# Another written order for the steps of the fused attention and feed-forward stage

## The chip, the cores and the metric

The kernel runs on one core of one Trainium2 chip. The metric is the device time of one execution in microseconds (us), as the median over several executions. A core has five engines that matter here: TensorE (PE in the profile; its weight loads stand apart as PEld), VectorE (DVE), ScalarE (ACT), GpSimd (POOL) and SyncE (SP, which issues DMAs). Each engine takes its instructions in the order in which they are written, and waits on semaphores for what the others produce.

## The reference

The input is one sequence of 2048 tokens with 128 channels. Four layers follow each other, each on the normalized sum so far: an oscillatory state space layer, a mixture of eight experts, a causal attention with 16 heads of 8 channels, and a block of six sub-layers of windowed attention and feed-forward. The last block takes two thirds of the time, and the change lies in it. Cut to what matters:

```python
def attn_layer(x, Wqkv, qs, ksc, Wo):            # HEADS 16, DIM_HEAD 64, WINDOW 32
    q, k, v = jnp.split(x @ Wqkv, 3, -1)         # then split into heads
    q = l2norm(q) * qs
    k = l2norm(k) * ksc
    q = q * cos * scale + rotate_half(q) * sin * scale
    k = k * cos * inv + rotate_half(k) * sin * inv
    out = local_attention(q, k, v)               # softmax over own and previous window of 32
    return out @ Wo

def ffn_layer(x, g, bln, W1, b1, W2, b2):
    xn = layernorm(x) * g + bln
    a, gate = jnp.split(xn @ W1 + b1, 2, -1)     # 341 channels each
    return a * gelu(gate) @ W2 + b2

for i in range(DEPTH):                           # DEPTH 6
    x = attn_layer(shift_tokens(x), ...) + x
    x = ffn_layer(shift_tokens(x), ...) + x
```

## The kernel before

The kernel has three earlier stages, which the change leaves alone, and `stage4`, which holds the six sub-layers. Stage 4 keeps the sequence transposed on the chip (channels on partitions, tokens along the free dimension) in two buffers, `s4[0]` and `s4[1]`, and cuts it into 16 tiles of 128 tokens. With six sub-layers that makes 96 tiles, numbered through by `t`. The work on a tile is cut into named steps, and every step is a small function. Some belong to each tile, some to each pair of tiles (`px0` to `px3`, `s`), some to each group of four (the feed-forward steps), and some to each sub-layer (`mm`, `mc0`, `mc1`).

The steps of a tile, in the order in which the data flows, with the engine that does each:

- `tab` (POOL): table of rotary factors. `ps00`, `ps01` (PE): the queries into a PSUM buffer of two banks; `ps10`, `ps11`: the keys into another.
- On the queries' buffer: `ra0` and `rb0` (DVE, multiply with the tables), `sq0` (ACT, squares). On the keys' buffer: `ra1`, `rb1`, `sq1`. `ss0`, `ss1` (DVE): sums of the squares. `rs0`, `rs1` (POOL): add the two rotary halves. `rn` (POOL, 12 small instructions): inverse norms. `kn` (POOL): scale the keys.
- `pt0`, `pt1` (PE): transpose queries and keys. `qT`, `kT` (ACT): copy them out of PSUM. `ca` (ACT): hand the last window of keys to the next tile.
- `sc0` to `sc3` (PE): scores. `sm`, `mx` (DVE): add the mask, negated row maxima. `nb` (POOL): scale these. `ex0`, `ex1` (ACT, eight exponentials each). `su`, `rc` (DVE): row sums and reciprocals. `nr` (POOL): scale. `tr` (DVE): transpose in blocks.
- `z0`, `z1` (PE): weights times inputs. `zc0`, `zc1` (ACT): copy out. `px0` to `px3` (PE, per pair): times the product of the value and output matrices, which `mm` (PE) and `mc0`, `mc1` (ACT) make once a sub-layer. `s` (DVE): add to the sequence.
- Per group of four tiles: `xk`, `xkc` transposed inputs for `z`; `xt`, `xs`, `fr`, `xn`, `xu`, `xb` the normalization; `ph00` to `ph21` (PE), `ge0` to `ge2` (ACT), `act0` to `act2` (DVE), `py0` to `py2` (PE) the feed-forward; `s2` (DVE) adds to the sequence; `st` stores, in the last sub-layer.

What sets the order is the list `steps`. It gives each step a lateness in units of one tile. Step `name` of tile `t` becomes a job at `t + lateness`; all jobs are sorted by that number and called one after the other:

```python
                    jobs.append((t + late, job))
            for _, job in sorted(jobs, key=lambda j: j[0]):
                job()
```

The engines' objects are wrapped (`InOrder`, line 67), so that no scheduler moves an instruction afterwards. For that reason nearly every instruction of stage 4 stands under line 67 in the profile, and is told apart by the tiles that it writes and reads. Steps by their tiles in the profile: `ra`: rot_a<-big,tab; `rb`: rot_b<-big,tab; `sq`: sq<-big; `ss`: ss<-sq; `ex`: sm<-sm,mx,rn; `rs`: rot_a<-rot_a,rot_b; `s`: s<-s,big; `sc`: big<-kT,qT; `z`: big<-at,xw; `px`: big<-zs,vo; `ps`: big<-wqk,s.

Three things tie the engines to this order beyond the data itself.

- PSUM buffers: the function `big` hands out four buffers of two banks, in the order in which they became free in the written order. `ps00`, `ps10`, `pt0`, `pt1`, `sc0`, `z0` (two), `px0` and the feed-forward steps take one each, and wait on the chip until the former user's last reader is done. A key buffer is held until its third reader (`sq`, `ra` or `rb`) is done.
- Readers of one PSUM buffer on different engines are put in the written order by semaphores: two reads of the same buffer by DVE and ACT do not overlap. In the order before, `sq0` is written after `ra0` and `rb0`, and its instruction waits for `rb0`; `rb1` is written after `sq1`, and waits for it.
- The remainder of stage 3: four jobs `left0` to `left3` at 1.2, 2.2, 3.1 and 3.4 finish tiles 4 to 7 of the sequence. The weights of sub-layer `l` are loaded by a job at `16 l - 3.5`, and the value and output matrices of the next one by the step `mm`.

Of the kernel before, what the change touches and what calls it, by code (L numbers as in the profile page):

```python
# [94 lines left out]
class Kernel:  # L95
# [885 lines left out]
    def stage4(self, x3, out):  # L981
        nc, tc, a = self.nc, self.tc, self.a
        with ExitStack() as ctx:
# [36 lines left out]
            st = [{} for _ in range(DEPTH * NT + 1)]  # L1020
# [426 lines left out]
            def of(f, *n):  # L1447
                return lambda t: f(t, *n)

            tiles = dict(  # L1450
                tab=tab, rn=rn, kn=kn, pt0=of(pt, 0), qT=qT, pt1=of(pt, 1), kT=kT, ca=ca, sm=sm,
                mx=mx, nb=nb, su=su, rc=rc, nr=nr, tr=tr,
# [11 lines left out]
            for n in range(3):  # L1464
# [6 lines left out]


            steps = [
                ("tab", 3.450), ("ps00", 4.422), ("ps01", 4.422), ("ra0", 4.460), ("rb0", 4.460), ("ps10", 4.543),
                ("ps11", 4.637), ("sq0", 4.715), ("sq1", 4.734), ("rb1", 4.919), ("ra1", 4.991), ("rs0", 5.208),
                ("ss1", 5.244), ("rs1", 5.279), ("ss0", 5.300), ("rn", 5.300), ("kn", 5.300), ("pt0", 5.484),
                ("qT", 5.484), ("pt1", 5.756), ("kT", 5.756), ("sc0", 6.172), ("sc1", 6.179), ("sc2", 6.179),
                ("sc3", 6.223), ("sm", 6.309), ("mx", 6.309), ("nb", 6.420), ("ca", 6.444), ("ex0", 7.153),
                ("ex1", 7.319), ("su", 7.446), ("rc", 7.719), ("xk", 7.750), ("xkc", 7.783), ("nr", 7.950),
                ("tr", 8.007), ("z0", 8.275), ("z1", 8.300), ("zc0", 8.364), ("zc1", 8.416), ("mm", 8.893),  # L1480
                ("px0", 9.005), ("px1", 9.005), ("px2", 9.005), ("px3", 9.160), ("mc1", 9.257), ("s", 9.267),
                ("mc0", 9.438), ("xt", 13.584), ("xs", 13.584), ("fr", 13.623), ("xn", 13.956), ("xu", 14.168),
                ("xb", 14.168), ("ph00", 14.404), ("ph01", 14.404), ("ge0", 14.404), ("ph10", 14.891),
                ("ph11", 14.891), ("ge1", 14.905), ("ph20", 14.917), ("ph21", 14.919), ("act0", 14.921),
                ("ge2", 14.924), ("py0", 15.002), ("act1", 15.154), ("act2", 15.165), ("py1", 15.394),
                ("py2", 15.394), ("s2", 15.415), ("st", 15.500),
            ]
            last = DEPTH * NT
            jobs = [(1.2, left0), (2.2, left1), (3.1, left2), (3.4, left3)]
# [126 lines left out]
```

## Time and profile before

| what | us |
|---|---|
| median of three executions | 2426.61 (2423.41 to 2428.54) |
| profiled execution, device time | 2425.9 |
| its span on the core | 2424.2 |
| first PE instruction of stage 4 | 782.1 |
| first `ps00` (tile 0) | 797.0 |
| `ra0` of tile 4, 16 and 95 | 850.8, 1043.7, 2340.5 |
| last add into the output | 2419.8 |
| one sub-layer in the steady part (16 tiles) | 262.8 |

In the second to fifth sub-layer every 16 tiles take 262.8 us, so a tile takes 16.43 us. The busy time of each engine in these 262.8 us: PE 246.9, DVE 222.0, ACT 209.3, POOL 201.1. Overlapping records are counted once, so that busy and idle time add up. The granted TensorE clock over the span is 0.95, and 0.98 in the steady part. DMA moves little there (its share is 0.04 at most).

How to read the views: the "windows" view gives the busy time of each engine in a stretch and, in brackets, the number of instructions. The groups of instructions give the busy time, the mean duration of one in nanoseconds, then the idle time of the engine just before them with who ended it. The timeline gives start, duration, engine and tiles.

### The profile page before, as it was taken

To read this page: it belongs to the slowest core of one execution; us is meant where nothing else is said; L and a number is where in the kernel's file an instruction comes from. 1 tells how busy PE (TensorE), PEld (TensorE's weight loads), DVE (VectorE), ACT (ScalarE), POOL (GpSimd) and SP (SyncE) were. 2 spreads that over 40 slices of the span, in tenths; PEclk is the share of its full clock that TensorE was granted. 3 is DMA by queue.
4 is the path that set the end of the run, shared out by engine and by line. 5 is a ranking of instruction groups with operands and counts; after the bars stand their busy time and mean duration, and the time that the engine had idled before them with its cause. 6 is when DMAs were issued, how large, how long until landed. Compare 5 with 4: busy or idle time off the path is not lost.

```text
span 2424.2 us, 61787 instructions
## 1 busy us (share of the span) xinstructions
PE 2158.5 (89%) x26188; PEld 1240.8 (51%) x26188; DVE 1880.0 (78%) x2808; ACT 1643.0 (68%) x3221; POOL 1394.1 (58%) x2122
## 2 busy tenths in 40 slices
PE   4677889999998699999998999999999999899997
PEld 3563333333333365556555655656555655555564
DVE  7666768777663688888888888888888888888873
ACT  3322445666665488788777877778878877787773
POOL 4244310011011688777777777777877777777770
PEclk8888989999998799999999999999999999999998
DMA  2000000000001000000000000000000000000000
GB/s 74 1 1 1 1 1 2 2 2 2 2 1 63 3 19 1 13 10 25 4 2 21 19 11 2 21 2 28 2 10 13 25 5 2 2 2 1 6 6 9
DMA packets 14134, 25.38 MB, mean 10 GB/s; under 512 B 1657, under 2 KB 10530, under 8 KB 13090
## 3 DMA queue, kind: packets, MB, share of 16 engines
q1 hardware_dynamic: 13276, 20.97, 2.7%
q8 instruction: 206, 3.38, 0.6%
q10 hardware_dynamic: 582, 0.46, 0.1%
q14 instruction: 70, 0.57, 0.1%
HBM read 20.37 MB, written 1.05 MB: 9 GB/s over the span
## 4 chain that ended last, share of the span: by engine, by line
PE 49%; DVE 33%; ACT 8%; issue 5%; POOL 4%; DMA 0%; POOLq 0%; DVEq 0%; ACTq 0%
PE big L67 31%; PE sc L67 9%; DVE mx L67 6%; DVE rot_a L67 5%; DVE rot_b L67 5%; PE av L67 5%; ACT sq L67 4%; DVE ss L67 3%; DVE sm L67 2%; DVE su L67 2%; DVE at L67 2%; DVE s L67 1%; ACT sm L67 1%; DVE act L67 1%; PE py L67 1%
## 5 line engine op out<-in xcount | busy, mean ns | idle before, releaser
L67 ACT ACTIVATE sm<-sm,mx,rn 128x64 f32<-128x64 f32 x1536 | 522.9, 436 | 0.3
L67 POOL TENSOR_TENSOR rot_a<-rot_a,rot_b 128x1024 f32<-128x1024 f32 x192 | 451.9, 2365 | 24.2 <-DVE rot_a L67 18.8
L67 DVE TENSOR_REDUCE mx<-sc 128x1 f32<-128x512 f32 (+3 forms) x640 | 354.9, 604 | 124.2 <-PE sc L67 117.2
L67 ACT ACTIVATE ex<-sc 128x512 f32<-128x512 f32 (+3 forms) x640 | 302.5, 536 | 204.2 <-PE sc L67 200.9
L67 PE MATMUL big<-wqk,s 128*128 128x512 f32 x768 | 374.7, 606 | 3.2 <-DVE sm L67 3.2
L67 PE MATMUL big<-zs,vo 128*128 128x256 f32 x1536 | 342.4, 381 | 16.2 <-ACT sq L67 14.8
L67 DVE TENSOR_TENSOR rot_b<-big,tab 128x1024 f32<-128x1024 f32 x192 | 234.2, 1220 | 143.8 <-ACT sq L67 142.3
L67 PEld LDWEIGHTS big<-zs,vo 128*128 128x128 f32 x1536 | 288.2, 190 | 58.7 <-ACT sq L67 19.5
L67 PE MATMUL sc<-qT,kT 32*128 32x512 bf16 (+3 forms) x1920 | 248.5, 353 | 24.6 <-DVE mx L67 16.3
L67 DVE TENSOR_TENSOR rot_a<-big,tab 128x1024 f32<-128x1024 f32 x192 | 233.7, 1217 | 44.1 <-PE big L67 43.4
L67 ACT ACTIVATE sq<-big 128x1024 f32<-128x1024 f32 x192 | 186.1, 1021 | 111.1 <-DVE rot_b L67 111.1
L67 PE MATMUL big<-at,xw 32*128 32x512 f32 x1536 | 233.7, 685 | 24.5 <-DVE at L67 24.4
L67 PEld LDWEIGHTS big<-ident,rot_a 128*128 128x128 f32 x1536 | 174.9, 141 | 139.9 <-POOL rot_a L67 63.3
L67 ACT COPY zs<-big 128x1024 f32<-128x1024 f32 x192 | 186.2, 1009 | 82.5 <-PE big L67 82.5
L67 PE MATMUL sc<-kT,qT 32*128 32x512 bf16 (+3 forms) x1920 | 232.3, 359 | 1.6 <-DVE krest L67 0.5
L67 PE MATMUL big<-ident,rot_a 128*128 128x128 f32 x1536 | 203.1, 275 | 33.8 <-POOL rot_a L67 29.1
L67 DVE TENSOR_REDUCE ss<-sq 128x16 f32<-128x1024 f32 x192 | 226.1, 1198 | 1.4
L67 POOL TENSOR_TENSOR sm<-sm,su 128x1024 f32<-128x1024 f32 x96 | 182.6, 1902 | 61.5 <-DVE su L67 61.5
L67 PEld LDWEIGHTS big<-wqk,s 128*128 128x128 f32 x768 | 135.2, 194 | 154.2 <-issue 139.5
L67 POOL TENSOR_SCALAR_AFFINE_SELECT ex<-ex 128x512 f32<-128x512 f32 x64 | 40.6, 635 | 272.3 <-ACT ex L67 272.0
L67 POOL TENSOR_TENSOR rot_a<-rot_a,rn 128x1024 f32<-128x1024 f32 x96 | 182.6, 1903 | 7.5
L67 PE MATMUL av<-ex,va 128*32 128x256 f32 (+1 forms) x2432 | 180.6, 378 | 4.9 <-POOL ex L67 3.5
(236 smaller groups left out, 3353.4 us busy)
## 6 DMA issues: line engine op xcount, KB each, us to landing
wqk<-in_L_ffn_Wqkv SPq DMA_DIRECT2D x12, 512.0 KB, 5.2
wvo<-in_wvo SPq DMA_DIRECT2D x6, 1024.0 KB, 5.5
w<-in_L_ffn_W SPq DMA_DIRECT2D x6, 341.0 KB, 7.2
x<-in_L_attn_hidden_states SPq DMA_DIRECT2D x4, 256.0 KB, 4.3
out<-act SPq DMA_DIRECT2D x4, 256.0 KB, 2.7
rot<-in_rot SPq DMA_DIRECT2D x1, 960.0 KB, 7.2
w<-in_L_ffn_W SPq DMA_DIRECT2D x12, 64.0 KB, 1.8
qks<-in_qks SPq DMA_DIRECT2D x6, 128.0 KB
```

The costliest lines, as they stand in the source:

```text
L67: return self._tc.keep_in_program_order(call(*args, **kw))
```

## The change

Only the list `steps` differs: the same 72 steps with other latenesses. No function, tile, instruction or DMA is added or removed; their order on each engine changes, and with it who waits for whom and which PSUM buffer is reused after which.

```diff
             steps = [
-                ("tab", 3.450), ("ps00", 4.422), ("ps01", 4.422), ("ra0", 4.460), ("rb0", 4.460), ("ps10", 4.543),
-                ("ps11", 4.637), ("sq0", 4.715), ("sq1", 4.734), ("rb1", 4.919), ("ra1", 4.991), ("rs0", 5.208),
-                ("ss1", 5.244), ("rs1", 5.279), ("ss0", 5.300), ("rn", 5.300), ("kn", 5.300), ("pt0", 5.484),
-                ("qT", 5.484), ("pt1", 5.756), ("kT", 5.756), ("sc0", 6.172), ("sc1", 6.179), ("sc2", 6.179),
-                ("sc3", 6.223), ("sm", 6.309), ("mx", 6.309), ("nb", 6.420), ("ca", 6.444), ("ex0", 7.153),
-                ("ex1", 7.319), ("su", 7.446), ("rc", 7.719), ("xk", 7.750), ("xkc", 7.783), ("nr", 7.950),
-                ("tr", 8.007), ("z0", 8.275), ("z1", 8.300), ("zc0", 8.364), ("zc1", 8.416), ("mm", 8.893),
-                ("px0", 9.005), ("px1", 9.005), ("px2", 9.005), ("px3", 9.160), ("mc1", 9.257), ("s", 9.267),
-                ("mc0", 9.438), ("xt", 13.584), ("xs", 13.584), ("fr", 13.623), ("xn", 13.956), ("xu", 14.168),
-                ("xb", 14.168), ("ph00", 14.404), ("ph01", 14.404), ("ge0", 14.404), ("ph10", 14.891),
-                ("ph11", 14.891), ("ge1", 14.905), ("ph20", 14.917), ("ph21", 14.919), ("act0", 14.921),
-                ("ge2", 14.924), ("py0", 15.002), ("act1", 15.154), ("act2", 15.165), ("py1", 15.394),
-                ("py2", 15.394), ("s2", 15.415), ("st", 15.500),
+                ("tab", -0.681), ("ps00", 0.000), ("ps01", 0.000), ("ra0", 0.049), ("sq0", 0.094), ("ss0", 0.186),
+                ("ps10", 0.205), ("ps11", 0.205), ("rb0", 0.219), ("sq1", 0.231), ("rb1", 0.231), ("ra1", 0.451),
+                ("rs0", 0.508), ("rs1", 0.561), ("ss1", 0.636), ("rn", 0.646), ("kn", 0.975), ("pt0", 1.054),
+                ("qT", 1.153), ("pt1", 1.490), ("kT", 1.505), ("ca", 1.688), ("sc0", 1.700), ("sc1", 1.875),
+                ("sc2", 1.907), ("sc3", 1.907), ("sm", 1.907), ("mx", 1.907), ("nb", 1.907), ("ex0", 2.171),
+                ("ex1", 2.935), ("su", 2.962), ("rc", 3.040), ("nr", 3.297), ("tr", 3.529), ("xk", 3.637),
+                ("xkc", 3.755), ("z0", 3.917), ("z1", 3.917), ("zc1", 3.988), ("zc0", 4.005), ("px0", 5.266),
+                ("px1", 5.453), ("mm", 5.620), ("mc1", 5.621), ("px2", 5.648), ("mc0", 5.681), ("px3", 6.291),
+                ("s", 6.475), ("xt", 11.567), ("xs", 11.976), ("fr", 12.088), ("xn", 12.298), ("xu", 12.664),
+                ("xb", 12.856), ("ph00", 13.295), ("ph01", 13.505), ("ge0", 13.539), ("act0", 13.542),
+                ("ph10", 13.556), ("ph11", 13.580), ("ph20", 13.620), ("ph21", 13.621), ("ge1", 13.630),
+                ("act1", 13.630), ("ge2", 13.631), ("py0", 13.643), ("py1", 13.645), ("act2", 13.813),
+                ("py2", 14.008), ("s2", 14.394), ("st", 14.494),
             ]
```

Folded into one tile's turn, and leaving out the steps that belong to groups, the orders on DVE and ACT are these; a number behind a step says how many tiles it lags behind the newest tile.

```
DVE before: su-3 ra0 rb0 rc-3 rb1 ra1 tr-3 ss1 ss0 sm-1 mx-1      (s-4 in every second turn, between ss1 and ss0)
DVE after:  rc-3 ra0 ss0 rb0 rb1 ra1 tr-3 ss1 sm-1 mx-1 su-2      (s-6 in every second turn, behind ra1)
ACT before: ca-2 qT-1 sq0 sq1 kT-1 ex0-2 ex1-2 zc0-3 zc1-3
ACT after:  zc0-4 sq0 qT-1 ex0-2 sq1 kT-1 ca-1 ex1-2 zc1-3
```

In the program as built after the change, `sq0` waits for `ra0`, `ss0` waits for `sq0`, and `rb1` waits for `sq1`. The first tiles' steps start at lateness 0 instead of 3.45, so that `left0` to `left3` stand between the steps of tiles 0 to 3, where they stood ahead of the first `tab` before.

## The prediction

> **What bounds the kernel now.** First the windows view: the stretch, its length, busy us and records of PE, PEld, DVE, ACT, POOL, the granted clock, DMA share, GB/s. The first row holds tiles 0 to 15, the second a steady sub-layer.
>
> ```profile
> 797.00:1041.00 244.00, 213.95 (x2805) 134.31 (x2803) 195.94 (x215) 179.67 (x344) 189.25 (x277) 0.92 0.03 11
> 1304.00:1567.00 263.00, 247.08 (x3117) 155.93 (x3114) 222.14 (x268) 209.26 (x398) 201.31 (x294) 0.98 0.04 12
> ```
>
> No engine is full: of 262.8 us PE is idle for 16 and DVE for 41. What bounds a tile's turn is therefore a ring of waits, and I count it on DVE, where each idle stretch has a named cause. The groups of DVE in that sub-layer show them (busy, mean ns, idle before, by whom):
>
> ```profile
> L67 DVE TENSOR_TENSOR rot_b<-big,tab 128x1024 f32<-128x1024 f32 x32 | 39.0, 1219 | 23.4 <-ACT sq L67 23.1
> L67 DVE TENSOR_TENSOR rot_a<-big,tab 128x1024 f32<-128x1024 f32 x32 | 38.9, 1217 | 7.1 <-PE big L67 7.0
> L67 DVE TENSOR_REDUCE ss<-sq 128x16 f32<-128x1024 f32 x32 | 37.7, 1198 | 0.2
> L67 DVE TENSOR_TENSOR s<-s,big 64x256 f32<-64x256 f32 x16 | 6.7, 420 | 8.4 <-PE big L67 8.3
> ```
>
> Per tile (divide by 16): `rb1` waits 1.46 for `sq1`, `ra0` 0.44 and `s` 0.52 for PE, `ss` next to nothing. DVE works 222.14/16 = 13.88 and stands 2.54: 16.43 a tile. Then the timeline, to see why `rb1` waits:
>
> ```profile
> 1386.16 1.02 ACT L67 COPY qT<-big 128x1024 f32<-128x1024 f32 x1
> 1390.42 2.77 ACT L67 ACTIVATE sm<-sm,mx,rn 128x64 f32<-128x64 f32 x8
> ...
> 1421.77 1.22 DVE L67 TENSOR_TENSOR rot_b<-big,tab 128x1024 f32<-128x1024 f32 x1
> 1423.02 1.94 ACT L67 ACTIVATE sq<-big 128x1024 f32<-128x1024 f32 x2 [1.79 <-DVE rot_b L67]
> 1425.06 1.23 DVE L67 TENSOR_TENSOR rot_b<-big,tab 128x1024 f32<-128x1024 f32 x1 [1.92 <-ACT sq L67]
> ```
>
> `rb0` ends at 1422.99 and ACT, idle for 1.79 although PE is long done with that buffer, starts `sq0` 0.03 later; both squares end at 1424.96 and `rb1` starts 0.10 later. So DVE and ACT take turns on the queries' and keys' buffers, in the written order, and every hand-over is paid in full. Before, ACT does both squares in one go between them.
>
> **The ring after the change.** It takes this apart. DVE runs `ra0 ss0 rb0 rb1`, and `ss0` needs `sq0`, which now waits for `ra0`. ACT runs `sq0 qT ex0 sq1`: eight exponentials and a copy now stand between the two squares, and `rb1` waits for the second. From the end of `ra0`, with back-to-back costs (two squares take 1.94, so the first costs 0.92; by the same overlap `qT` costs 0.92 and `ex0` 2.67):
> - `sq0` starts at 0.03 and ends at 1.05, `ss0` starts at 1.15: DVE stands 1.15.
> - `rb1` starts at 0.03 + 0.92 + 0.92 + 2.67 + 1.02 + 0.10 = 5.66. DVE has only `ss0` and `rb0` for that time, 1.13 + 1.22 from 1.15 on, so it is done at 3.50 and stands 2.16.
>
> That is 3.31 standing in place of `rb1`'s 1.46. The 0.96 for PE at `ra0` and `s` I cost at nothing, because DVE is now the later one: counted from `ra0`, a plain turn is 1.22 + 5.66 to `rb1`, then seven DVE steps at 1.16 and `rc`, 15.2 in all; `z` can end at about 14 (`tr` ends at 10.3, `sc` and `z` take 1.4 and 1.9 by their starts in the timeline), and `px3`, which `s` needs, is issued a turn's fraction ahead. If that cover went, 0.96 a tile would return. With 0.07 for record overlap that a wait undoes: 13.88 + 3.31 + 0.07 = 17.26.
>
> **The turn with the feed-forward** (one in four). `ph10` takes the PSUM buffer that `ra1` reads last, free at 9.2 in that turn. Behind it on PE stand `ph11`, `ph20`, `ph21`, `py0`, `py1` and then `sc`: six steps at 0.85 (four `ps` records cover 1.71 to the next start) and 1.4, so `sc` ends at 15.7. DVE reaches `sm` after `rb1 ra1 s tr act0 act1 ss1 act2`, at 14.4. It waits 1.3, or 0.33 per tile. Queued behind it are `mx`, `su`, `rc` and the next `ra0`. Once a sub-layer `mm` (2.06 on PE) and `mc1` now fall into such a turn; between 0 (hidden) and 2.8/16 = 0.18 I take 0.15, as everything behind `ph11` stands on the path there. Sum 17.74.
>
> **The clock.** The rows show 0.98 while PE's longest idle stretches are 1.7 us, and 0.92 in the filling stretch where they are longer. After, PE stands about 3 us ahead of `ph10` and nearly 4 ahead of `xk`. Bounds: 0, and 6.5% more on 15.4 us of PE, 1.0; on the path it counts in the feed-forward turn and a little in `xk`'s, so 0 to 0.3 per tile. I take 0.15, the middle: 17.9 (17.35 to 18.5 with all bounds).
>
> [...]
>
> **POOL, PSUM and DMA.** POOL has 12.6 us of work in a turn of 17.9: `rn` follows `ss1`, `kn` ends some 2.5 us into the next turn, `nr` 4.5 and `tr` needs it at 9; hidden. PE's new waits for buffers (`pt0` for `zc1`, `px0` for `qT`, `xk` for `ra1`, `sc` for `s` or `s2`) end ahead of `sm`'s turn on DVE outside the feed-forward turn; a microsecond beyond costs 0.25 per tile. The weights' DMAs stay where they are in number, now 2.8 tiles (50 us) ahead of `tab` instead of 7; they land in 5 to 7 us. The load of the next matrices on SP waits for `mm` as before; nothing queued behind it is due within 100 us. No cost.
>
> **The start.** The remainder of stage 3 now runs between the first tiles.
>
> ```profile
> 781.25 0.91 SPq L994 DMA_DIRECT2D rot<-in_rot  x2
> 797.12 1.17 ACT L67 COPY s<-big 64x512 f32<-64x512 f32 x2 [11.08 <-PE big L67]
> 800.60 1.22 DVE L67 TENSOR_TENSOR rot_a<-big,tab 128x1024 f32<-128x1024 f32 x1 [3.62 <-PE big L67]
> ```
>
> Before, tile 0's first matmul stands on PE behind all of the remainder (that copy is its last step), at 797.0. After, `ra0` of tile 0 waits for the rotary table's first piece (issued 781.25, 5.1 to land) and `tab` (0.73): 787.2, 13.4 earlier. Tiles 0 to 3 then take about 8, 10, 15 and 18 us, with five us of the remainder on DVE among them; `ra0` of tile 4 comes at 838 instead of 850.8: -12.5. Tiles 4 to 15 are 12 turns at 15.2, five `s` at 0.8 and the first group's feed-forward, 11: 197 against 192.9 (850.8 to 1043.7): +4. Tile 16 is then 8.5 early.
>
> **The drain.** From `ra0` of tile 95 to the end are 83.7 now. After: a turn of 18, two of 10 without `ra` to `rs`, 9 to `zc0` of tile 95, 7 for `px`, 9 until the previous group's feed-forward has left PE, 25 for the last group (as now, 2399.3 to the end) come to 88. I take +3 (-9 to +13).
>
> **Sum.** Tile 16 to 95 takes 1296.8 now, 79 turns of 16.415. After 79 x 17.9 = 1414: +117. With -8.5 and +3: +112, span 2536. The profiled execution was 2425.9 for a span of 2424.2, and 0.7 below the median, so 2.4 is added: **2538 us**, 4.6% slower.
>
> **The rivals.**
> - *Heavier:* the halved clock, or PSUM hand-overs that come back to DVE. For it: feed-forward and `xk` turns have no slack. Against: plain turns have one to three us. A turn of 18.7 gives 79 x 2.3 = 181 and about 2602. Chance 0.13.
> - *Milder:* `sc` of the feed-forward turn and `mm` find cover, and the clock stays: a turn of 17.3 gives +70, a span of 2489, 2491 with the median. For it: the floor of 17.26 is all that is certain. Chance 0.14.
> - *Faster:* ACT isn't held at all. The place is `sq0`: were it free to run as soon as `ps01` is done, ACT could run a turn ahead and DVE would find `sq0` and `sq1` ready. PE's 15.4 would bound a turn, and the time would be 2427 - 13 - 92 x 1.0 = 2322. It decides from the point where DVE's standing falls below the present 2.54 a tile. Against: the built program has the wait for `ra0`, and the timeline shows such a wait paid. For it: the longer distances between most other steps would take all other waits away. Chance 0.05.
> - *No gain or loss*, the start's 13 balancing a turn of 16.6, or the order on the engines hardly differing: the engine orders do differ, so 0.02.
>
> The forecast (a turn of 17.5 to 18.5) has 0.66. What this kernel's runs can tell from no change is about 0.2%, or 5 us. Faster 0.05, same 0.02, slower 0.93. The range reaches from the milder case to near the heavier one: 2485 to 2592.
>
> **What would show it.** Right: DVE's `ss` with some 1.1 us idle before every `ss0`, owed to ACT `sq`; `rot_b` with about 2.1 per tile owed to `sq`; `rot_a` and `s` without waits for PE; `sm` waiting for PE in every fourth turn; 286 us per sub-layer; `ra0` of tile 0 near 787. Wrong: `sq` without waits for DVE, or `ex0` not between the squares; a sub-layer under 275 or over 297 us; `ra0` waiting for PE in most turns, which would mean that PE, not this ring, bounds.

## The result, and the profile after

The changed kernel takes **2621.06 us** (2616.66 to 2622.75, four runs) against 2426.34 for the kernel before beside it: a ratio of 1.0801 (95% interval 1.0782 to 1.0819). It is slower, as forecast, but by 195 us where 112 were forecast, and outside the range (2485 to 2592). The profiled span grew from 2424.2 to 2614.9.

| stretch, from `ra0` to `ra0` | before | after | difference | forecast |
|---|---|---|---|---|
| start of the span to tile 0 | 800.6 | 787.3 | -13.3 | -13.4 |
| tile 0 to 16 | 243.1 | 266.1 | +23.0 | +4.9 |
| tile 16 to 95, 79 turns | 1296.8 | 1471.5 | +174.7 | +117 |
| tile 95 to the end | 83.7 | 90.0 | +6.3 | +3 |

The page's groups of instructions of the changed kernel, over all 96 tiles (busy, mean ns of one, then the idle time ahead of them and who ended it):

```profile
L67 DVE TENSOR_TENSOR rot_b<-big,tab 128x1024 f32<-128x1024 f32 x192 | 234.1, 1220 | 207.2 <-ACT sq L67 207.2
L67 DVE TENSOR_REDUCE ss<-sq 128x16 f32<-128x1024 f32 x192 | 231.0, 1203 | 104.1 <-ACT sq L67 104.1
L67 DVE TENSOR_TENSOR rot_a<-big,tab 128x1024 f32<-128x1024 f32 x192 | 230.7, 1202 | 16.6 <-PE big L67 8.6
L67 ACT ACTIVATE sq<-big 128x1024 f32<-128x1024 f32 x192 | 195.5, 1019 | 185.7 <-DVE rot_a L67 182.0
L67 PE MATMUL big<-xc,w 128*128 128x512 f32 (+1 forms) x288 | 159.3, 683 | 55.4 <-DVE rot_a L67 54.6
```

Divide by 96: DVE stands 2.16 for `sq1` at `rb1` and 1.08 for `sq0` at `ss0`. The wait for PE at `rot_a` is almost gone. The fourth line is the other half of the ring: `sq0` waits for `ra0`. The last line is the wait that the forecast saw ahead of `ph10`: PE stands 54.6 us for `ra1`, which reads that PSUM buffer last. The sum held it only through the time at which `sc` ends.

The windows of two steady sub-layers (length, busy us of PE, PEld, DVE, ACT and POOL, granted clock):

```profile
1348.00:1645.00 297.00, 255.97 (x3111) 161.12 (x3110) 221.42 (x258) 210.14 (x397) 198.19 (x288) 0.93 0.04 11
1645.00:1942.00 297.00, 254.84 (x3114) 161.31 (x3113) 224.37 (x268) 211.47 (x398) 201.18 (x294) 0.94 0.03 11
```

A sub-layer takes 297 instead of 263, DVE works as long as before, and the clock fell from 0.98 to 0.93 or 0.94. The mean turns of the profiled executions, by the tile's number modulo four, say where it sits (the feed-forward's `ph` and `py` stand in turn 1 after and mostly in turn 2 before):

| | turn 0 | 1 | 2 | 3 | mean |
|---|---|---|---|---|---|
| before | 13.67 | 18.15 | 17.48 | 16.36 | 16.42 |
| after | 16.76 | 21.80 | 16.90 | 19.06 | 18.63 |

The timeline of turn 57, which holds a feed-forward (`ra0` at 1814.1; start, duration, engine, tiles, idle before):

```profile
1819.86 1.02 PE L67 MATMUL big<-xc,w 128*128 128x512 f32 x2
...
1823.44 5.37 PE L67 MATMUL big<-xc,w 128*128 128x512 f32 x8 [2.56 <-DVE rot_a L67]
...
1827.31 0.75 DVE L67 SCALAR_TENSOR_TENSOR act<-big,vec,ge 128x512 f32<-128x512 f32 x1 [1.19 <-ACT ge L67]
...
1828.65 1.88 PE L67 MATMUL big<-act,w 128*128 128x512 f32 x4
...
1830.46 1.48 PE L67 MATMUL big<-kT,qT 64*32 64x64 f32 x128
...
1831.98 1.22 DVE L67 TENSOR_TENSOR sm<-big,mask 128x1024 f32<-128x1024 f32 x1 [1.45 <-PE big L67]
```

`ph10` starts 9.3 after `ra0`, as forecast (9.2). But the eight matmul records from there take 5.37 for `ph10` to `ph21`, not 4 x 0.85: the clock is at half from 1824.11 for 3.41 us. PE does not stand again between there and the end of `sc`. So `ge1` is late, `act1` waits 1.19, and `sc` ends at 17.9 where 15.7 was forecast. Turn 59 holds `xk`, the transposed inputs for `z` (the texts on record call it the value projection, and its turn is the value turn below). It has the same pattern (`ra0` at 1852.6):

```profile
1857.28 0.66 PE L67 MATMUL big<-ident,s 128*128 128x128 f32 x4
1861.92 1.94 PE L67 MATMUL big<-ident,s 128*128 128x128 f32 x8 [3.98 <-DVE rot_a L67]
1863.78 1.88 PE L67 MATMUL big<-kT,qT 64*32 64x64 f32 x128
```

`xk` stands 3.98 for `ra1`'s buffer, then takes 1.94 where the kernel before needs 1.04; the clock is at half from 1861.66 for 3.41 us.

### The profile page after: what moved, and what is told of

Its sections match the earlier page's. It is cut to its first block, busy times and chain, and to the rows that moved or that the text cites. A ratio compares the mean times of both kernels' runs of the same rounds, so it can differ in the third digit from the quotient of the medians.

```text
span 2614.9 us, 62058 instructions
## 1 busy us (share of the span) xinstructions
PE 2209.2 (84%) x26188; PEld 1272.1 (49%) x26188; DVE 1895.6 (72%) x2808; ACT 1655.9 (63%) x3221; POOL 1394.7 (53%) x2122
## 4 chain that ended last, share of the span: by engine, by line
DVE 36%; PE 31%; ACT 23%; issue 5%; POOL 4%; DMA 1%; DVEq 0%; POOLq 0%; SPq 0%; ACTq 0%
PE big L67 14%; ACT sm L67 10%; DVE rot_a L67 8%; PE sc L67 8%; DVE mx L67 7%; ACT sq L67 7%; PE av L67 5%; DVE rot_b L67 4%; DVE su L67 4%; ACT qT L67 4%; DVE sm L67 3%; DVE at L67 2%; DVE s L67 1%; DVE fh L67 1%; PE py L67 1%
## 5 line engine op out<-in xcount | busy, mean ns | idle before, releaser
L67 ACT ACTIVATE sm<-sm,mx,rn 128x64 f32<-128x64 f32 x1536 | 532.3, 436 | 0.3
L67 PE MATMUL big<-zs,vo 128*128 128x256 f32 x1536 | 371.4, 391 | 40.4 <-ACT qT L67 40.2
L67 ACT ACTIVATE sq<-big 128x1024 f32<-128x1024 f32 x192 | 195.5, 1019 | 185.7 <-DVE rot_a L67 182.0
L67 PE MATMUL sc<-qT,kT 32*128 32x512 bf16 (+3 forms) x1920 | 248.5, 351 | 24.6 <-DVE mx L67 16.3
L67 DVE TENSOR_TENSOR rot_a<-big,tab 128x1024 f32<-128x1024 f32 x192 | 230.7, 1202 | 16.6 <-PE big L67 8.6
L67 PE MATMUL big<-at,xw 32*128 32x512 f32 x1536 | 214.8, 666 | 24.1 <-DVE at L67 22.4
L67 PEld LDWEIGHTS big<-ident,rot_a 128*128 128x128 f32 x1536 | 181.0, 142 | 86.7 <-issue 39.3
L67 PE MATMUL big<-xc,w 128*128 128x512 f32 (+1 forms) x288 | 159.3, 683 | 55.4 <-DVE rot_a L67 54.6
L67 PE MATMUL big<-kT,qT 64*32 64x64 f32 x12288 | 157.7, 246 | 35.9 <-DVE rot_a L67 14.0
```

What stands on the lines that cost most here:

```text
L67: return self._tc.keep_in_program_order(call(*args, **kw))
```

## The experiments

The 17 kernels compare with the kernel before on the same chip. "Turn" is the mean over tiles 16 to 95 of the one profiled execution; idle times "a tile" are means over the same tiles. Only numbers in the list `steps` were altered, but for e3.

| run | us | ratio (95% interval) | turn | turns 0, 1, 2, 3 |
|---|---|---|---|---|
| e1 | 2511.5 | 1.0364 (1.0327 to 1.0401) | 17.45 | 16.5, 20.4, 15.6, 17.3 |
| e2 | 2688.4 | 1.1081 (1.1053 to 1.1110) | 19.28 | |
| e3 | 2594.5 | 1.0694 (1.0671 to 1.0718) | 18.22 | 16.6, 20.8, 16.8, 18.7 |
| e4 | 2422.5 | 0.9986 (0.9974 to 0.9998) | 16.42 | |
| e5 | 2615.7 | 1.0776 (1.0754 to 1.0798) | 18.60 | 17.1, 21.5, 16.8, 19.0 |
| e6 | 2515.5 | 1.0353 (1.0325 to 1.0381) | 17.50 | 17.1, 19.2, 16.4, 17.3 |
| e7 | 2508.5 | 1.0345 (1.0309 to 1.0381) | 17.33 | 15.8, 19.3, 16.9, 17.3 |
| e8 | 2506.2 | 1.0337 (1.0306 to 1.0369) | 17.36 | 16.0, 19.3, 16.9, 17.2 |
| e9 | 2590.0 | 1.0668 (1.0646 to 1.0690) | 18.29 | 17.2, 20.2, 17.0, 18.7 |
| e10 | 2549.8 | 1.0512 (1.0496 to 1.0527) | 17.77 | 17.4, 19.2, 18.2, 16.3 |
| e11 | 2557.9 | 1.0546 (1.0530 to 1.0561) | 17.88 | 17.5, 19.4, 18.2, 16.4 |
| e12 | 2450.5 | 1.0091 (1.0067 to 1.0114) | 16.75 | 17.5, 17.8, 18.2, 13.3 |
| e13 | 2424.5 | 0.9989 (0.9979 to 0.9998) | 16.48 | 17.6, 17.9, 17.4, 13.0 |
| e14 | 2565.7 | 1.0563 (1.0540 to 1.0586) | 18.09 | 18.0, 19.0, 18.5, 16.7 |
| e15 | 2607.2 | 1.0739 (1.0720 to 1.0758) | 18.61 | 18.4, 22.4, 16.3, 17.3 |
| e16 | 2424.2 | 0.9990 (0.9978 to 1.0003) | 16.47 | 17.6, 17.9, 17.4, 12.9 |
| e17 | 2448.8 | 1.0094 (1.0078 to 1.0110) | 16.78 | 17.5, 17.9, 17.4, 14.2 |

### The ring: e1 and e2

e1 puts the squares back together in the changed list:

```diff
-("ss0", 0.186) ("rb0", 0.219) ("sq1", 0.231) ("qT", 1.153) ("ex0", 2.171)
+("ss0", 0.600) ("rb0", 0.050) ("sq1", 0.206) ("qT", 1.207) ("ex0", 2.240)
```

> The changed order, but with both squares between rb0 and rb1 again (DVE: ra0 rb0 rb1 ra1, ss0 beside ss1; ACT: sq0 sq1 qT ex0). DVE's standing for ACT falls from 1.10 + 2.19 us a tile to one wait of about 2.07, 1.2 less. If the ring alone costs, and PE's clock and the feed-forward turn stay as they are, a tile takes 17.35 instead of 18.58, and the time is 2621 - 92 x 1.2 = about 2510. If the clock's drops hang on the ring (ra1 ends 2.5 us earlier in the turn, so PE's idle stretches ahead of ph10 and xk shrink from 2.6 and 4.0 to about 0.1 and 1.5), the halved clock goes too, and the time is 2400 to 2450. If the slowness comes from other steps of the order, it stays over 2580.

The groups of DVE in e1:

```profile
L67 DVE TENSOR_TENSOR rot_b<-big,tab 128x1024 f32<-128x1024 f32 x192 | 233.9, 1218 | 203.2 <-ACT sq L67 172.9
L67 DVE TENSOR_REDUCE ss<-sq 128x16 f32<-128x1024 f32 x192 | 223.6, 1196 | 0.0
```

The wait at `ss0` is gone and 110 us with it. Half-clock time fell from 2.20 to 0.82 us a tile (0.65 before): `ra1` then gives its buffer back at 6.8 instead of 9.2, and PE's stand ahead of `ph` fell from 0.66 to 0.03 a tile. So the time is that of the first case, about 2510, but the clock went up as in the second; that the first case's sum fits is in part luck. e1 still stands 86 us above the kernel before.

e2 makes the same ring in the list before:

```diff
-("sq0", 4.715) ("ss0", 5.300) ("rb0", 4.460) ("ex0", 7.153) ("kn", 5.300)
+("sq0", 4.461) ("ss0", 4.462) ("rb0", 4.463) ("ex0", 6.500) ("kn", 5.320)
```

> The order before, with the ring alone put in: sq0 and ss0 between ra0 and rb0, and ex0 between qT and sq1 ahead of sq1's reader. Ring theory: DVE stands 1.15 + 2.15 a tile for ACT, in place of 1.46 for ACT and 0.96 for PE, so a turn is 17.2 to 17.5 without any knock-on: 2424 + 96 x 0.9 = about 2510 (2495 to 2530). If PE's idle stretches grow past 3 us here too, its clock falls and the time is 2530 to 2600. If the ring isn't what costs, 2425 to 2450.

It cost 263 us, more than any theory gave. The two waits are there (1.09 at `ss0`, 1.92 at `rb1`), but at the shorter distances of that list the late rotations come back in the same turn: in turn 56 `sc0` stood 4.3 us on PE, and DVE waited 0.93 a tile at `ra0`, 0.78 at `s` and 0.39 at `sm`. The clock fell too: half-clock time rose from 0.65 to 3.33 us a tile, more than in the changed kernel. How much of the 263 us is the clock and how much the shorter distance between the ring and the later steps was not tried.

### The clock and the buffers: e3 and e9

e3 is the changed order with repeated matmuls that change no result, so that PE is busy where it stood: the second `ph0` three times more, four matmuls into the unused half of `xt`'s buffer, the last `ps1` twice more in every second tile.

```diff
+                if s and h and t % 2 == 0:
+                    for _ in range(2):
+                        pe.matmul(st[t]["ps", s][:, h], ...)
```

> The changed order, with PE kept busy in its three idle stretches by repeated matmuls that change nothing (ph01 three times more in the feed-forward turn, four into the unused half of xt's buffer in xk's turn, ps11 twice more in every second turn). No wait is taken away. Clock theory: half-clock time falls from about 25 us a sub-layer to under 8, xk takes 1.0 instead of 1.9, ph10 and ph11 1.0 instead of 1.47, and a turn of four tiles loses 2.5 to 4 us: 2621 - 23 x 3 = about 2550 (2530 to 2570). If the clock doesn't matter, the time stays within 10 us of 2621 or rises.

A window of a sub-layer of e3:

```profile
1340.00:1631.00 291.00, 279.31 (x3200) 168.91 (x3199) 224.34 (x267) 210.49 (x397) 200.68 (x293) 0.99 0.04 11
```

The clock was 0.99, half-clock time 0.09 us a tile where the changed kernel has 2.20 (35 us a sub-layer), and the turn fell by 0.41: 32 us over 79 turns. In all the medians fell by 27 and the profiled executions by 20, as the drain got 14 longer; that lies between the two cases of the expectation. Half-clock time of 2.20 us costs PE 1.1 us of work a tile, but only 0.4 of it reached the end. No wait was taken away and the added matmuls take time of their own, so this is the least that the clock costs.

e9 keeps the order of every engine in a turn and changes only which buffer goes to whom: `ph10` and `xk` take the one that `kT` gives back.

```diff
-("ra1", 0.451) ("s", 6.475)
+("ra1", 0.506) ("s", 6.507)
```

> The changed order with two numbers altered, ra1 0.506 for 0.451 and s 6.507 for 6.475: in a turn every engine keeps its order, and only the accumulator buffers are handed round otherwise, so that ph10 (feed-forward turn) and xk (value turn) take the buffer that kT gives back and no longer the one that ra1 gives back. In the changed kernel's trace both stand until ra1 ends: ph10 of turn 57 from 6.8 to 9.4 us while kT ended at 7.7, xk of turn 59 from 5.3 to 9.3 while kT ended at 7.6. Theory A (the late ra1, held back by the ring, keeps a buffer that these two need; this is what the forecast left out of the feed-forward and value turns): both start about 1.6 us earlier, TensorE is granted more clock there, those two turns shorten by 0.8 to 1.6 us each, 0.4 to 0.8 us per tile over 79 turns: 2555 to 2590 us. Theory B (the turns are set by the order on the engines, whoever holds the buffers): 2615 to 2625.

PE in turn 57 of e9 (`ra0` at 1811.6):

```profile
1817.36 1.02 PE L67 MATMUL big<-xc,w 128*128 128x512 f32 x2
1819.27 3.70 PE L67 MATMUL big<-xc,w 128*128 128x512 f32 x8 [0.88 <-ACT kT L67]
1823.65 1.98 PE L67 MATMUL big<-act,w 128*128 128x512 f32 x4 [0.68 <-DVE act L67]
1825.57 1.48 PE L67 MATMUL big<-kT,qT 64*32 64x64 f32 x128
```

`ph10` now waits for `kT`, 0.88 instead of 2.56, the eight records take 3.70 instead of 5.37, and `sc` ends at 15.5. The feed-forward turns fell from 21.80 to 20.22, the value turns from 19.06 to 18.74, the time by 31 us. Theory A holds for the feed-forward turn; in the value turn most of it stayed although `sm` no longer waited there. Half-clock time fell only from 2.20 to 1.73 us a tile: it went out of the feed-forward turn (2.1 to 0) and came up in turn 0 (1.2 to 4.0), which grew by 0.4.

### The start: e4

All latenesses of the kernel before, less 4.422, so that its first tiles start among `left0` to `left3` as after the change:

> The order before with 4.422 taken from every lateness, so that the first tiles' steps start at 0 and the remainder of stage 3 runs between them, as in the changed order; the order in the steady part is the same. Start theory: ra0 of tile 0 moves from 800.6 to 787, tiles 1 to 3 lose some of it to the remainder's steps, and the time falls by 3 to 13 us: 2411 to 2422. If the start is worth nothing, within 3 us of 2426.

Tile 0 came 12 us earlier, tile 16 still 6, and the time fell by 0.14%, 2.5 us. In the changed kernel the same start lost all of it, and tile 16 came 9.7 later than in the kernel before. Turn 3 took 19.8 in both (13.6 in the kernel before), ahead of `left3`. Against e4 the changed kernel lost 4.2 us in tiles 0 to 3, most of it in turn 1 (18.2 for 14.9), and 12.8 in tiles 4 to 15, where its turns are the longer ones anyway.

### What is left without the ring: e5 to e8

e5 takes `py1` out of `sc`'s way in the changed order (`py1` 14.007 for 13.645):

> The changed order with one number altered: the projection py1 stands at 14.007, beside py2 in the next turn, instead of the step ahead of sc. Theory A (in the feed-forward turn the end is set on TensorE's list: sc stands behind py1, which waits for ge1 and act1): sc ends about 0.85 us earlier in every fourth turn, the wait of sm in that turn falls from 1.5 to about 0.7, some 0.2 us per tile over 79 turns: about 2604 us (2590 to 2612). Theory B (the feed-forward turn is set by VectorE's own list alone, and sc is not what the turn waits for): 2617 to 2625.

The median fell by 5.4 us, to a value between the two theories, but the medians of the kernel before beside the two lie 1.3 apart and the intervals overlap: small at most. e6 to e8 start from e1:

```diff
e6 +("py1", 14.007) ("act0", 13.637) ("act1", 13.639) ("mm", 5.510) ("mc1", 5.520) ("mc0", 5.530)
e7  e6 and +("xk", 2.950) ("xkc", 3.010)
e8  e7 and +("su", 3.060) ("rc", 3.061)
```

> The changed order with the squares together as in the run e1_squares_together (2511 us, 17.445 per turn), and beside it the feed-forward's waits opened: py1 at 14.007, act0 at 13.637 and act1 at 13.639 (behind ss1, so that VectorE reaches them when ge0 and ge1 are done), mm, mc1 and mc0 at 5.510 to 5.530. Theory A (what was left of the 195 us lies in the feed-forward turn's order: act0 waiting for ge0, sc behind py1): that turn falls from 20.44 to 17.9 to 18.5, 0.5 to 0.6 us per tile: 2450 to 2470 us. Theory B (the turn is as long as TensorE's own work with ph and py and the clock it gets; order does not matter): 2500 to 2515.

> As e6_squares_and_feed_forward, and the value projection xk and its copy xkc are moved from ahead of sc to 2.950 and 3.010. Theory A (xk stands ahead of sc in its turn and costs that turn what it takes): the turn with xk falls by about 0.5 us, 0.12 per tile, about 10 us below e6. Theory B (xk is hidden beside VectorE anyway): within 3 us of e6.

> As e7_and_value_turn, and su and rc of the softmax are moved between rb0 and rb1, into the 2.1 us in which VectorE stands for the second square. Theory A (VectorE's ring of busy and standing time sets the turn): the stand ahead of rb1 falls from 2.14 to about 0.75, 1.4 us per tile, until TensorE's own 15.4 us bound it: 2320 to 2400. Theory B (the ends of the turn wait for TensorE or for the softmax's later steps, which now come later): 2400 to 2450, with new standing time ahead of pn or sm.

Each opened the wait that it aimed at, and none shortened the sum. In e6 the feed-forward turn fell from 20.44 to 19.19, and turn 2, which took over `py1`, and turn 0 grew by 0.8 and 0.7. In e7 the value turn did not shorten; turn 0 fell by 1.3, turn 2 grew by 0.5, and the 7 us between the medians lie within the intervals. In e8 the stand at `rb1` fell from 2.36 to 0.95, and `ra0` waited 1.22 for PE in its place. Theory A fell in e6 and e8, and e8 lies above the range of its theory B too; in e7 the turn that theory A names did not move. The reading that fits is that waits of one engine were removed in a turn that another engine held.

### Two changes that need each other: e10 to e15

e10 brings all four `px` into one turn and e11 does the same for `xt` to `xu`, from e8:

```diff
e10 +("px3", 5.660) ("s", 5.670)
e11  e10 and +("xt", 12.100) ("xs", 12.225) ("fr", 12.228)
```

> As e8_and_stand_filled (2506 us, 17.36 per turn), with px3 at 5.660 and s at 5.670, so that all four px stand in one turn and their buffer is held for about 10 us instead of over 20. Theory A (what keeps that order above the kernel before is TensorE standing for buffers that are held longer, px0 standing 0.56 us per tile among it): TensorE's standing falls by 0.3 to 0.6 us per tile: 2460 to 2485. Theory B (buffers are not what it stands for; the turns' work is then only less evenly spread): 2500 to 2540.

> As e10_px_in_one_turn, with xt 12.100, xs 12.225 and fr 12.228, so that xt's buffer is given back in the same turn (held about 7 us instead of 24), and xs stands in VectorE's wait ahead of rb1. Theory A: px0 finds a buffer at once, another 0.2 to 0.5 us per tile: 2425 to 2470. Theory B (buffers do not decide): within 10 us of e10.

Both were slower than e8, and e10 lies above both its theories. PE's stand ahead of `px` fell as expected (0.59 to 0.27 to 0.15 us a tile), but that ahead of `sc` grew (0.73 to 1.14 to 1.33). PE, then ACT in turn 59 of e11 (`ra0` at 1818.7):

```profile
1821.02 1.04 PE L67 MATMUL big<-ident,rot_a 128*128 128x128 f32 x8
1827.58 2.05 PE L67 MATMUL big<-kT,qT 64*32 64x64 f32 x128 [5.52 <-ACT kT L67]
```

```profile
1823.87 2.76 ACT L67 ACTIVATE sm<-sm,mx,rn 128x64 f32<-128x64 f32 x8
1826.53 1.00 ACT L67 COPY kT<-big 128x1024 f32<-128x1024 f32 x1
```

This turn has little for PE to do, and it could be short. But `pt1` is done at 1822.06, and ACT does the eight exponentials of `ex0` first, then `kT`. So `sc`, `z` and the next `ps` can't start before 8.9, and no turn can be much shorter than 15.3. The kernel before has `kT` ahead of `ex0`, and turns of 13.67. e12 restores that in e11, e14 in e8, e15 in e1:

```diff
e12  e11 and +("ex0", 2.640) ("act0", 13.560)
e13  e12 and +("xk", 3.520) ("xkc", 3.632)
e14  e8 and  +("ex0", 2.640) ("act0", 13.560)
e15  e1 and  +("ex0", 2.520)
```

> As e11_xt_in_one_turn (2558 us), with ex0 at 2.640, so that ScalarE copies kT ahead of ex0 as in the kernel before, and act0 at 13.560. In e11 kT ended at 8.8 in every turn, sc0 stood for it 5.5 us in the turn that holds neither feed-forward nor px, and that turn was 15.4 long where the kernel before needed 13.6. Theory A (kT behind ex0 sets a floor of about 15.4 under every turn, so the short turns can't give back what the long ones take): that turn falls to 13 to 13.6, the feed-forward turn to 16 to 17, about 1 us per tile: 2430 to 2490. Theory B (something else holds the turns): 2540 to 2560.

> As e12_keys_ahead_of_ex0, with xk 3.520 and xkc 3.632: the value projection goes from a turn that TensorE fills with px to the one in which it stands. Theory A (in the px turns TensorE's own work sets the length): that turn falls by about 1.0 us and the short turn grows by less than 0.5, so 0.1 to 0.25 us per tile: 10 to 20 us below e12. Theory B: as e12, within 5.

> As e8_and_stand_filled (2506 us, px in two turns, xt held over a turn), with ex0 at 2.640 and act0 at 13.560. Theory A (kT's place is the floor): only the turn 59 of e8 stood for kT (2.9 us), and xs on VectorE then bounds it at about 15.3; with the feed-forward turn down by 0.5: 0.3 us per tile, 2470 to 2490. Theory B: 2500 to 2512.

> As e1_squares_together (2511 us), with ex0 alone moved to 2.520, behind kT. Theory A (kT's place by itself makes up the 86 us): 2430 to 2460. Theory B (it is a floor that only binds once the other waits are gone; in e1 only one turn in four stands for kT, 0.8 us): 2495 to 2512.

The same turn of e12 (ACT):

```profile
1764.08 1.04 ACT L67 COPY kT<-big 128x1024 f32<-128x1024 f32 x1
1764.98 2.77 ACT L67 ACTIVATE sm<-sm,mx,rn 128x64 f32<-128x64 f32 x8
```

With `kT` done 6.2 after `ra0` instead of 8.8 the turn is 12.7 long, and e12's theory A holds. Four medians side by side:

| | `kT` behind `ex0` | `kT` ahead of `ex0` |
|---|---|---|
| `px` over two turns | 2506 (e8) | 2566 (e14) |
| `px` in one turn | 2550 (e10), 2558 (e11) | 2451 (e12) |

Either alone costs 44 to 60 us, both together gain 56. (e12 has e11's `xt` too, worth 8 the other way, and e12 and e14 also move `act0`.) e15 moves `ex0` alone, and loses 96 us against e1. Where that loss comes from shows on ACT in its turn 60 (`ra0` at 1859.6):

```profile
1863.84 1.02 ACT L67 COPY qT<-big 128x1024 f32<-128x1024 f32 x1
1870.38 1.01 ACT L67 COPY kT<-big 128x1024 f32<-128x1024 f32 x1 [5.53 <-PE big L67]
1871.29 2.76 ACT L67 ACTIVATE sm<-sm,mx,rn 128x64 f32<-128x64 f32 x8
```

In a turn with `px`, PE does `px0` and `px1` ahead of `pt1`; here it stood 3.69 for the buffer that the squares held, and then took 6.38 for them, where two `px` take 3.62 in the kernel before. `kT` waits 5.53 for that, the exponentials queue behind it, and `su` waits 1.35 for them. With `px` in every turn that wait sits in turns that would else be short; with `px` gathered it sits in turns of 17.5 to 18.2, which PE's own work fills anyway, and the others get short. e15's and e14's expectations (2512 at most, where 2607 and 2566 came) missed this: both named the gain at `sc` and not who stands behind `kT` on ACT. e13 moves one more piece of PE's work into the short turn and is level with the kernel before.

### At the floor: e16 and e17

```diff
e16  e13 and +("ge1", 13.590) ("act1", 13.595)
e17  e16 and +("xt", 11.600)
```

> As e13_and_value_in_short_turn (2424.5 us), with ge1 13.590 and act1 13.595: VectorE does act1 ahead of the squares' sums instead of behind them. In e13 z0 of the feed-forward turn stood from 11.6 to 12.0 for the buffer that act1 gives back at 11.9. Theory A (TensorE's stand for that buffer sets the turn): 0.4 us in every fourth turn, 0.1 per tile: 2412 to 2420 us. Theory B (the next turn takes it back): 2421 to 2428.

> As e16_act1_earlier, with xt at 11.600: its transposes go from the turn that TensorE fills with px to the short turn, in which TensorE stands 1.6 us for kT. Theory A: the px turn falls by about 0.6 us plus the 0.8 that xt stood there, the short one grows by less than 0.4: 0.15 to 0.3 us per tile, 12 to 24 us below e16. Theory B (xt's buffer, then held over a turn, makes px0 wait as it did in e10): within 5 us of e16, or above it.

e16: the wait went, the time stayed. In both runs `z1` ends at 14.6 in that turn; what paces it is open. e17 is 25 us slower: turn 3 grew from 12.9 to 14.2, and the `px` turn 0 gave back only 0.1; theory B, though by a wait that it hadn't named (PE stood 1.0 ahead of the next `ps`). No version here beats the kernel before by more than 0.2%: e4, e13 and e16 lie 0.10 to 0.14% below it.

The groups of DVE in e13, and its windows (compare 263 and 0.98 before):

```profile
L67 DVE TENSOR_TENSOR rot_a<-big,tab 128x1024 f32<-128x1024 f32 x192 | 234.2, 1220 | 117.6 <-PE big L67 106.5
...
L67 DVE TENSOR_TENSOR rot_b<-big,tab 128x1024 f32<-128x1024 f32 x192 | 234.1, 1219 | 78.9 <-ACT sq L67 73.0
```

```profile
1293.00:1557.00 264.00, 245.61 (x3119) 156.12 (x3118) 222.96 (x269) 209.89 (x399) 201.56 (x297) 0.99 0.04 12
1557.00:1820.00 263.00, 246.06 (x3117) 156.42 (x3116) 222.69 (x269) 209.48 (x398) 201.44 (x296) 0.99 0.04 12
```

DVE's standing has moved from `rot_b` to `rot_a`: it now waits for PE, which itself is idle for 1.0 us a tile, as in the kernel before.

## Why the forecast was right in direction and wrong in size

The forecast fell 83 us short: 58 in the 79 turns, 18 in the start, 3 in the drain, and 4 because the profiled execution lay further below its median than the forecast allowed.

**The ring: right.** Forecast 1.15 at `ss0` and 2.16 at `rb1`, measured 1.10 and 2.19 a tile in the steady part. "I cost at nothing, because DVE is now the later one" held for `ra0` (0.07) and `s` (0.01). e1 shows that the ring, with the late buffers and the clock that hang on it, is 110 of the 195 us.

**The clock: the step that failed.** "I take 0.15, the middle" is the term that was mis-sized. e3 shows at least 0.41 a tile, 32 us where the sum had 12, so it is at least 20 of the 58. The forecast had the cause in hand (`ph10` waits for `ra1`'s buffer until 9.2) and then priced the six steps behind it at the full clock. The trace of turn 57 shows what that did: 1.8 of the 2.2 us by which `sc` came late are the eight `ph` records at half the clock. In e9, where `ph10` starts 1.6 earlier and PE keeps the full clock, `sc` ended at 15.5 and `sm` waited 1.0 (forecast 1.3).

On DVE most of the shortfall of a turn (18.63 for 17.9) stands in two waits. These are its waits in the changed kernel from 1500 to 2400 us, 48.3 tiles (in total, times, longest):

```profile
DVE sm L67 <- PE big L67: 31.0, 28, 2.0
DVE act L67 <- ACT ge L67: 18.7, 9, 4.4
```

`sm` waited 0.64 a tile for PE, and in the value turn as well as in the feed-forward turn. `act` waited for `ge` and PE, 0.47 a tile over tiles 16 to 95, and had no term of its own. Together that is 1.11, where the sum had 0.63 (0.33 for `sm`, 0.15 for `mm`, 0.15 for the clock). In e3 the two fell to 0.39 and 0.22, in e9 to 0.46 and 0.14.

**The value turn: missed.** The forecast let PE's new waits for buffers end in time "outside the feed-forward turn", `xk` for `ra1` among them. In the trace `xk` stood 3.98, took 1.94 instead of 1.04 with the clock at half from 1861.66 to 1865.07, and `sm` waited 0.8. So "No cost" for PE's new waits for buffers was the second step that failed. These turns took 19.06 in the mean; 15.2 for a plain turn, 0.8 for `s` and 1.87 for `xs` would give 17.9. e9 gave back 0.3 of that. In e9's turn 59 `xs` took 2.5 instead of 1.8, as its last small instruction took 0.74 instead of 0.17; why wasn't tried.

**The start: wrong sign.** `ra0` of tile 0 came at 787.3 (forecast 787.2). But tiles 0 to 3 took 60.5 us where 51 were added up. In turn 0 PE stood 7.1 for `rs0` of tile 0, and the clock was at half from 789.87 to 813.76; turn 1, with four `ps` records at 3.78 instead of 1.88, took 18.2 instead of 10. In turn 3 PE stood 7.0 ahead of `left3`, and the turn took 19.8 instead of 18. Tiles 4 to 15 took 205.6, not 197. **The drain** was +6.3, within its bounds.

**The rivals.** "Heavier", with a turn of 18.7 and 2602, was what happened in the turns (18.63), and the halved clock that it named is a shown part of it (0.65 us a tile at half the clock before, 2.20 after); the 19 us to 2621 lie in the start and the rest. It had a chance of 0.13. "Faster" needed ACT to be free of `ra0`; `sq0` waited 182.0 us for `rot_a`.

**What the forecast didn't ask.** e1's other 86 us are not a term of the sum that was off, since the sum was made from the changed order's own waits. e13 takes them back, and its last steps, from e8's 2506 to 2424.5, are `kT`'s place together with the spread of `px`, `xt` and `xk`. The edits of e6 to e8 stand in e13 too, and no run leaves them out again. Which part of e1's loss belongs to which alone can't be said, because the parts don't add.

## What to carry to other kernels

When a wait moves, follow the buffer as well as the data: a reader that ends 2.4 us later (9.2 us after `ra0` for 6.8 in e1) keeps a PSUM buffer, and the engine that needs it stands. In turn 57 PE stood 2.56 us for it, and 0.67 us after it went on its clock was at half. In an in-order schedule on several engines, a wait taken away alone may be worth nothing, and two moves that lose alone may win together, so look in each turn for the engine that holds it, and try moves in pairs. Before moving a step ahead on an engine, name what it waits for and who is queued behind it.

## What the runs showed of the hardware

In the traces of the kernel before and of the changed one the half-clock stretches (35 and 68 over the whole span) begin whole multiples of 3.41 us apart. In the steady part (tiles 16 to 95) the kernel before has 10 of them, of 3.41 or 6.83 us, and the changed one 39, of 3.41, 6.83 or 10.24 us.

In the kernel before, PE's idle time in the 3.41 us just ahead of these ten starts was 1.93 to 2.03 us in sum. In one of them PE stood 0.30 and then 1.73, until 1705.07, and the clock was at half from 1705.13 for 6.83 us. In five of them the longest single pause was 1.1 to 1.2. The other stretches of 3.41 us there, counted in the same steps, at the full clock and with the full clock after them, held 1.73 at most, and in some of these it was a single pause of 1.73. So in that trace the sum tells the two apart, and the longest pause does not.

In the changed kernel the 3.41 us ahead of the 39 starts held 1.99 to 3.41; those of turn 57 held 2.56, until 1823.44, and the half clock began at 1824.11. Those that kept the full clock held 1.96 at most. PE's ends are modelled in the profile, so these sums are rough.
